# The opening of layer 0: fewer zero transfers, tables and statistics issued earlier

## The chip, the cores and the metric

The kernel runs on one core of a Trainium2 chip. The metric is device time in microseconds (us) of one execution, as the median of several runs. The core's engines are called PE (matrix products), DVE (vector), ACT (scalar) and POOL (GpSimd); SP only issues transfers. ACT and POOL issue transfers too. Sixteen DMA engines carry what these queues issue.

## The reference

The program is four residual layers over an image `x` of shape 2 x 192 x 96 x 96. Before each layer a group norm without weights is taken of each image. Only the beginning of layer 0 matters here:

```
def _gn(v, G=32, eps=1e-5):                      # per image, 32 groups of 6 channels
    return (g - mean) / sqrt(var + eps)
xr   = conv1x1(_gn(x), w_reduce, b_reduce)       # 192 -> 180 channels
offs = conv1x1(xr, w_offset, b_offset)           # 180 -> 360 channels: (y, x) shifts of samples
f_w  = deform_conv2d(xr, offs[:, :180], ...)     # 3x3, samples xr at shifted places
f_h  = deform_conv2d(xr, offs[:, 180:], ...)
x    = x + conv1x1(attention-weighted sum of f_w and f_h)
```

Layers 1 to 3 (a Laplacian with a 1x1 convolution, a two-way WKV scan, a state space scan) follow and are the same in both kernels.

## The kernel before

Layer 0 handles the two images one after the other. For each image it needs the group norm's scale and bias, so it must first read the whole image for statistics. Then the first projection, `reduce0`, makes for each of 72 tiles of 128 pixels the 180 channels and the 360 offsets in one product, and writes both to device memory: the pixels into `xp_d`, a frame of 106 x 106 pixels of 194 floats with zeros around the 96 x 96 picture, and the offsets into `o_d`, with zero rows at both ends. After that, `near0` samples and convolves image 0; image 1's projection is interleaved with that ("aside").

The order of the beginning, as the program states it in `layer0`:

1. `stats_of(x, 0, 0)`: six loads of 96 x 2 x 1536 floats on SP, 36 `bn_stats` on DVE (L127). `gn` (L95 to L109) makes scale and bias of them.
2. `reduce_constants`: loads of the projection's weights (L76), a transposed and fused weight `wall` (L197 to L238), and the zeros: DVE clears the tile `zero` (L240), and ACT's queue sends it to device memory, for each image two transfers into `o_d` with 97 rows each (L246), one transfer for each of the ten zero lines of `xp_d`, 106 rows of 776 bytes each (L251), and two of 96 rows for the left and right margins (L252, L256).
3. `reduce0` of image 0: the tile's load on SP (L269), the normalization on DVE (L114), four products on PE (L286), the bias added on DVE into `xk` (L296 to L300), and five transfers of `xk` on ACT's queue (L306, L314). `xk` has four buffers. The products' PSUM pool `r0p` has three.
4. `stats_of(x, 0, 1)` and `gn` for image 1.
5. `near_constants`: small tables made on DVE by chains of operations on 128 x 1 values (L352 to L402), with ramps from POOL (L339), the load `sb_b_off`, and the store of a table `where` to `at_d` (L408). It also holds the loads of the convolution's weights `wd`, `wl` on POOL's queue (L439).
6. `near0` of image 0. It starts with loads of `raw` from `o_d` (L488), windows `xw` from `xp_d` on POOL's queue (L543, 16 transfers for a tile), `u` = `raw` + table (L498), the hat functions `h` on POOL and ACT (L525, L532, L534) and their products `sp` on DVE (L555). From the first `sp` on, DVE works nearly without a break.

A tile framework turns this into one instruction stream for each engine. It orders outside `near0` by its own priorities, so independent instructions may be moved ahead. Pools that are opened one after the other use the same memory: the first instruction on a new pool's tile waits until the old pool's last readers, transfers included, are done. Every transfer that SP or ACT issues takes one of eight completion semaphores in turn; a transfer with the same semaphore as an earlier one is issued after the earlier one has landed.

Of the kernel before, what the change touches and what calls it, by code (L numbers as in the profile page):

```python
# [6 lines left out]
F32 = mybir.dt.float32  # L7
# [4 lines left out]
PSUM = bass.MemoryType.PSUM  # L12
# [4 lines left out]
B, C, H, W = 2, 192, 96, 96  # L17
# [5 lines left out]
NS = 2 * G * KK  # L23
PITCH = 106
FRAME = 4
CW = 194
# [35 lines left out]
class Net:  # L62
# [52 lines left out]
            out, x, sc[:, k : k + 1], bi[:, k : k + 1], ALU.mult, ALU.add  # L115
        )

    def stats_of(self, src, layer, b):
        nc, tc = self.nc, self.tc
        stats = self.new_stats(layer, b)  # L120
        with tc.tile_pool(name=f"st{layer}{b}", bufs=4) as sb:
            for n in range(0, N512, 3):
                xt = sb.tile([CH, 2, 3 * 512], F32, name="xt")
                nc.sync.dma_start(out=xt, in_=halves(src[b])[:, :, n * 512 : (n + 3) * 512])
                for i in range(3):
                    for k in range(2):
                        nc.vector.bn_stats(  # L127
                            stats[:, k, n + i, :], xt[:, k, i * 512 : (i + 1) * 512]
                        )
        return stats  # L130

    def layer0(self, x, out):
        nc, tc, ins = self.nc, self.tc, self.ins
        new = [self.new_stats(1, b) for b in range(B)]
        with ExitStack() as ctx:
            wp = ctx.enter_context(tc.tile_pool(name="w0", bufs=1))
            xp_d, o_d, f_d, u_d, top = [], [], [], [], []
            for b in range(B):  # L140
                xp_d.append(self.dram.tile([PITCH, PITCH, CW], F32, name=f"xp_d{b}"))
                o_d.append(self.dram.tile([OB + HW + OA, 2 * NS], F32, name=f"o_d{b}"))
                f_d.append(self.dram.tile([2, CM, HW], F32, name=f"f_d{b}"))
                u_d.append(self.dram.tile([NT * LT, 2 * NS], F32, name=f"u_d{b}"))
                top.append(wp.tile([P, 8], F32, name=f"top{b}"))
            at_d = self.dram.tile([NT * LT, 4], F32, name="at_d")
            far = wp.tile([1, B], I32, name="far")
            sums = [self.dram.tile([2, CM], F32, name=f"sums_d{b}") for b in range(B)]
            with tc.tile_pool(name="wn0", bufs=1) as wn:
                gns = [self.gn(0, 0, self.stats_of(x, 0, 0))]  # L150
                wall, bias = self.reduce_constants(wn, xp_d, o_d)
                with tc.tile_pool(name="r0", bufs=4) as sb, tc.tile_pool(
                    name="r0p", bufs=3, space=PSUM
                ) as ps:
                    for _ in self.reduce0(
                        x[0], gns[0], wall, bias, xp_d[0], o_d[0], sb, ps, "pr", nc.scalar
                    ):
                        pass
                gns.append(self.gn(0, 1, self.stats_of(x, 0, 1)))
                con = self.near_constants(wn, at_d)  # L160
                with tc.tile_pool(name="r1", bufs=2) as sb:
                    aside = (x[1], gns[1], wall, bias, xp_d[1], o_d[1], sb)
                    self.near0(0, xp_d[0], o_d[0], u_d[0], f_d[0], sums[0], far, top[0], con, aside)
                self.near0(1, xp_d[1], o_d[1], u_d[1], f_d[1], sums[1], far, top[1], con)
            for b in range(B):
                rv = nc.values_load(far[0:1, b : b + 1], min_val=0, max_val=1)
                with tc.If(rv > 0):
                    self.far0(b, xp_d[b], o_d[b], f_d[b], sums[b])
            we = ctx.enter_context(tc.tile_pool(name="we0", bufs=1))
            wex = self.load(  # L170
                "w_exp", [MH, 2, C], ins["w_exp"].rearrange("(k p) o -> p k o", k=2), we
            )
            bex = self.load("b_exp", [CH, 2], pool=we)
            wat = self.load(
                "w_attn", [MH, 2, 2], ins["w_attn"].rearrange("(k p) o -> p k o", k=2), we
            )
            bat = self.load("b_attn", [P, 2], rows_of(ins["b_attn"], P), we)
            for b in range(B):
                few = (top[b], at_d, u_d[b], xp_d[b])
                self.expand0(b, x, out, f_d[b], sums[b], few, wex, bex, wat, bat, new[b])  # L180
        return new

    def reduce_constants(self, wn, xp_d, o_d):
# [5 lines left out]
        with tc.tile_pool(name="wr0", bufs=1) as wr, tc.tile_pool(  # L189
            name="wrp0", bufs=2, space=PSUM  # L190
        ) as ps:
            wred = self.load_halves("w_red", CM, wr)
            bred = self.load("b_red", [MH, 2], pool=wr)
            row = self.load("b_red_row", [P, CM], rows_of(ins["b_red_row"], P), wr)

            for k in range(2):
                nc.vector.tensor_copy(  # L197
                    wall[:, k, :CM].rearrange("p (e q c) -> p e q c", e=2, c=CG),
                    wred[:, k].rearrange("p (q e c) -> p e q c", e=2, c=CG),
                )  # L200
            nc.vector.tensor_copy(
                bias[:, :CM].rearrange("p (e q c) -> p e q c", e=2, c=CG),
                row.rearrange("p (q e c) -> p e q c", e=2, c=CG),
            )

            raw = self.load(
                "w_off", [MH, 2, 2 * NS], ins["w_off"].rearrange("(k p) o -> p k o", k=2), wr
            )
            woff = wr.tile([MH, 2, 2 * NS], F32, name="woff")
            for k in range(2):  # L210
                for a in range(2):
                    for cv in range(2):
                        nc.vector.tensor_copy(
                            woff[:, k].rearrange(
                                "p (t a q c e) -> p a c t q e", t=KK, a=2, c=2, e=2
                            )[:, a, cv],
                            raw[:, k].rearrange(
                                "p (a c q e t) -> p a c t q e", a=2, c=2, t=KK, e=2
                            )[:, a, cv],
                        )  # L220
            for k in range(2):
                back = wr.tile([MH, 2, CH], F32, name="back")
                for m in range(2):
                    pt = ps.tile([P, 2 * NS], F32, name="pt")
                    nc.tensor.transpose(
                        pt[:MH, :CH], wred[:, k, m * MH : (m + 1) * MH], self.ident[:CH, :CH]
                    )
                    nc.vector.tensor_copy(back[:, m], pt[:MH, :CH])
                pt = ps.tile([P, 2 * NS], F32, name="pt")
                for m in range(2):  # L230
                    nc.tensor.matmul(pt[:CH], back[:, m], woff[:, m], start=m == 0, stop=m == 1)
                nc.vector.tensor_copy(wall[:, k, CM:], pt[:CH])
            many = wr.tile([MH, 2, P], F32, name="many")
            nc.vector.tensor_copy(many, bred.unsqueeze(2).to_broadcast([MH, 2, P]))
            pt = ps.tile([P, 2 * NS], F32, name="pt")
            for m in range(2):
                nc.tensor.matmul(pt, many[:, m], woff[:, m], start=m == 0, stop=m == 1)
            nc.vector.tensor_copy(bias[:, CM:], pt)  # L238
            zero = wr.tile([PITCH, 8 * NS], F32, name="zero")
            nc.vector.memset(zero, 0.0)  # L240
            F = FRAME
            end = PITCH - F - W
            for b in range(B):

                for lo, n in ((0, 2 * OB), (HW, OB + OA)):
                    nc.scalar.dma_start(  # L246
                        out=o_d[b][lo : lo + n].rearrange("(p r) c -> p (r c)", p=97),
                        in_=zero[:97, : n // 97 * 2 * NS],
                    )
                for y in (*range(F), *range(F + H, PITCH)):  # L250
                    nc.scalar.dma_start(out=xp_d[b][y], in_=zero[:, :CW])  # L251
                nc.scalar.dma_start(  # L252
                    out=xp_d[b][F : F + H, :F, :].rearrange("y x c -> y (x c)"),
                    in_=zero[:H, : F * CW],
                )
                nc.scalar.dma_start(  # L256
                    out=xp_d[b][F : F + H, F + W :, :].rearrange("y x c -> y (x c)"),
                    in_=zero[:H, : end * CW],
                )
# [1725 lines left out]
```

## Time and profile before

| | us |
|---|---|
| median of 3 runs (lowest to highest) | 12206.34 (12203.41 to 12206.52) |
| the profiled execution | 12226.28 |
| its span | 12224.5 |
| PE busy, share of the span | 10189.2, 83% |
| DVE busy | 9584.8, 78% |
| ACT busy | 6563.0, 54% |
| POOL busy | 6938.6, 57% |

The shares are averages over all four layers. What the change touches lies in the first 480 us, under 4% of the span, so it is read there, by stretches of the timeline. In the page's 40 slices this is the first slice and half of the second: PE has 3 tenths of the first and 5 of the second, against 9 in the slices after it.

### The profile page before, as it was taken

How to read it: one execution, taken by the hardware profiler on the slowest of the kernel's cores; microseconds unless marked ns; L12 is line 12 of the kernel's file. 1: busy time of each engine (PE TensorE's matmuls, PEld its weight loads, DVE VectorE, ACT ScalarE, POOL GpSimd, SP SyncE). 2: the span in 40 equal slices, each digit the busy share in tenths (PEclk: the TensorE clock that was granted, in tenths of full speed). 3: DMA queues.
4: the chain of work that ended last, by engine and by line, in shares of the span. 5: the costliest groups of instructions: out<-in, count | busy, mean ns of one | idle time of the engine just before them, and what ended most of it. 6: DMA issues, size and time to landing. Idle time of an engine off the chain costs nothing. (4 is left out here: it accounts for less than half of the span.)

```text
span 12224.5 us, 231723 instructions
## 1 busy us (share of the span) xinstructions
PE 10189.2 (83%) x89389; PEld 5830.4 (48%) x89389; DVE 9584.8 (78%) x10919; ACT 6563.0 (54%) x12866; POOL 6938.6 (57%) x6899
## 2 busy tenths in 40 slices
PE   3599999998999999967767777778888888888887
PEld 2488888887888888852222222222222222222222
DVE  3777777776777777765688777679889899888988
ACT  0366666665766666630026433356565656656565
POOL 0366666765666666631247433356666666666666
PEclk9899999999999999978867777789899898898989
DMA  4534444432333333334322111111111111111111
GB/s 107 93 93 96 96 95 96 99 94 71 83 89 91 92 91 92 91 94 127 101 92 97 55 43 50 38 43 44 45 41 46 39 44 45 41 45 40 44 45 38
DMA packets 596759, 875.84 MB, mean 72 GB/s; under 512 B 237184, under 2 KB 322492, under 8 KB 594624
## 3 DMA queue, kind: packets, MB, share of 16 engines
q1 hardware_dynamic: 373448, 659.98, 20.4%
q0 software_dynamic: 103808, 133.18, 5.1%
q10 hardware_dynamic: 118392, 67.73, 1.9%
q8 instruction: 714, 11.70, 0.4%
q14 instruction: 397, 3.25, 0.1%
HBM read 423.24 MB, written 187.60 MB: 50 GB/s over the span
## 5 line engine op out<-in xcount | busy, mean ns | idle before, releaser
L1849 POOL TENSOR_TENSOR bu<-du,bb 128x512 f32<-128x512 f32 x1728 | 2235.2, 1308 | 1293.5 <-DVE h L1852 1286.1
L1856 PE MATMUL acc<-hc,ident 128*128 128x512 f32 x3456 | 1939.2, 677 | 652.0 <-DVE hc L1855 652.0
L1852 DVE TENSOR_TENSOR_SCAN h<-da,state,bu 128x512 f32<-128x512 f32 x1632 | 2030.1, 1274 | 240.5 <-ACT da L1847 199.0
L555 DVE TENSOR_TENSOR sp<-h 128x2304 f32<-128x2304 f32 x790 | 2161.7, 2769 | 19.9 <-ACT h L534 19.9
L579 ACT COPY st<-pt 128x512 f32<-128x512 f32 (+1 forms) x2370 | 1217.7, 516 | 1306.3 <-PE pt L571 1236.9
L577 DVE COPY st<-pt 128x512 f32<-128x512 f32 x1580 | 1062.0, 687 | 981.8 <-PE pt L571 965.9
L571 PE MATMUL pt<-ident,sp 128*128 128x128 f32 x14220 | 1678.8, 276 | 126.7 <-DVE sp L555 79.0
L525 POOL TENSOR_TENSOR h<-u,step 128x1152 f32<-128x1152 f32 (+1 forms) x474 | 1208.0, 2562 | 816.5 <-DVE u L498 468.7
L571 PEld LDWEIGHTS pt<-ident,sp 128*128 128x128 f32 x14220 | 1565.1, 142 | 214.5 <-issue 89.1
L1856 PEld LDWEIGHTS acc<-hc,ident 128*128 128x128 f32 x3456 | 630.2, 203 | 1874.5 <-DVE hc L1855 1497.2
L543 POOL DMA_DIRECT2D xw<-xp_d x2500 | 1389.4, 633 | 179.5 <-PE pt L618 83.5
L1847 ACT ACTIVATE da<-dl,sb_A_log 128x512 f32<-128x512 f32 x1728 | 1184.4, 687 | 4.0 <-POOL dl L1834 0.7
L1855 DVE TENSOR_TENSOR hc<-h,cc 128x512 f32<-128x512 f32 x1728 | 1117.3, 678 | 21.9 <-DVE h L1852 0.5
L618 PE MATMUL pt<-st,xw 64*32 64x288 f32 (+1 forms) x30000 | 1074.0, 366 | 72.4 <-ACT st L579 26.6
L1853 ACT COPY state<-h 128x1 f32<-128x1 f32 x1728 | 321.4, 190 | 1496.8 <-DVE h L1852 1496.4
L639 ACT COPY val<-pt 128x288 f32<-128x288 f32 (+1 forms) x3132 | 985.1, 398 | 209.0 <-PE pt L618 204.2
L686 PE MATMUL pf<-more,wl 54*64 54x128 f32 (+1 forms) x17064 | 957.6, 268 | 11.2 <-DMA more<-val 10.2
L686 PE MATMUL pf<-main,wd 126*64 126x128 f32 (+1 forms) x17064 | 962.3, 270 | 0.6
L686 PEld LDWEIGHTS pf<-main,wd 126*64 126x64 f32 x17064 | 889.9, 137 | 140.4 <-issue 136.4
L686 PEld LDWEIGHTS pf<-more,wl 54*64 54x64 f32 x17064 | 919.6, 136 | 47.7 <-issue 33.5
L618 PEld LDWEIGHTS pt<-st,xw 64*32 64x32 f32 x30000 | 539.6, 106 | 478.8 <-ACT val L639 169.8
L1844 PE MATMUL cc<-xd,pick 16*128 16x512 f32 x1152 | 710.5, 699 | 0.0
(309 smaller groups left out, 13505.0 us busy)
## 6 DMA issues: line engine op xcount, KB each, us to landing
main<-val SPq DMA_DIRECT2D x2016, 81.0 KB
bb<-br SPq DMA_DIRECT2D x576, 256.0 KB
more<-val SPq DMA_DIRECT2D x1728, 40.5 KB
xw<-xp_d POOLq DMA_DIRECT2D x2500, 26.0 KB
xt<-x_d SPq DMA_DIRECT2D x108, 384.0 KB
u_d<-u SPq DMA_DIRECT2D x158, 180.0 KB
raw<-o_d SPq DMA_DIRECT2D x156, 180.0 KB
half<-half_d SPq DMA_DIRECT2D x54, 512.0 KB
```

The costliest lines, as they stand in the source:

```text
L525: nc.gpsimd.tensor_tensor(hs, u[:, :, 8 * KK * l : 8 * KK * l + n].unsqueeze(3).to_broadcast([P, 2, n, WS]), con["step"].unsqueeze(1).unsq ...
L543: nc.gpsimd.dma_start(out=xw[e * WN : (e + 1) * WN, i], in_=xp_d[y : y + WS, x : x + WS, e * CM // 2 : e * CM // 2 + XW],)
L555: nc.vector.tensor_tensor(sp.rearrange("p s (y x) -> p s y x", x=WS), hy.unsqueeze(3).to_broadcast([P, n, WS, WS]), hx.unsqueeze(2).to_bro ...
L571: nc.tensor.transpose(pt[:, q], sp[:, 2 * (q0 + q) : 2 * (q0 + q) + 2].rearrange("p e w -> p (e w)"), self.ident,)
L579: nc.scalar.copy(st[:, q0 : q0 + m], pt[:, :m])
L618: nc.tensor.matmul(pvs[e][lane : lane + 32, j * w : (j + 1) * w], xw[e * WN : (e + 1) * WN, win, g * CG : g * CG + 32], sts[pair][e * WN : ...
L686: nc.tensor.matmul(to, wt[:, m * CO : (m + 1) * CO], took.rearrange("p h (r c) -> p h r c", c=columns), start=first and l == 0 and t == 0, ...
L1847: nc.scalar.activation(da, dl[:, d], AF.Exp, scale=nA[:, d, n : n + 1])
L1849: nc.gpsimd.tensor_tensor(bu, du[:, d], bb, ALU.mult)
L1852: nc.vector.tensor_tensor_scan(h, da, bu, init, ALU.mult, ALU.add)
L1855: nc.vector.tensor_tensor(hc, h, cc, ALU.mult)
L1856: nc.tensor.matmul(acc[d], self.ident, hc, start=n == 0, stop=n == NST - 1)
```

## The change

Three things are edited.

- The ten zero lines of `xp_d` are cleared with two transfers for each image. The tile `zero` becomes 97 x 10282 floats (it was 106 x 1440), and the lines 0 to 3 go out as 8 rows of 10282 floats, the lines 100 to 105 as 12 rows.
- `near_constants` is called after the first image's statistics and ahead of its `gn`.
- `stats_of` becomes a generator that yields after each load with its six `bn_stats`. The second image's statistics are advanced from inside the loop over `reduce0`, every thirtieth yield (ten tiles) from the twentieth on, and their loads have two buffers instead of four. The PSUM pool of the projection gets six buffers instead of three.

```diff
-    def stats_of(self, src, layer, b):
+    def stats_of(self, src, b, stats):
         nc, tc = self.nc, self.tc
-        stats = self.new_stats(layer, b)
-        with tc.tile_pool(name=f"st{layer}{b}", bufs=4) as sb:
+        with tc.tile_pool(name=f"st{b}", bufs=4 - 2 * b) as sb:
             for n in range(0, N512, 3):
...
-        return stats
+                yield
...
-                gns = [self.gn(0, 0, self.stats_of(x, 0, 0))]
+                first = self.new_stats(0, 0)
+                for _ in self.stats_of(x, 0, first):
+                    pass
+                con = self.near_constants(wn, at_d)
+                gns = [self.gn(0, 0, first)]
                 wall, bias = self.reduce_constants(wn, xp_d, o_d)
                 with tc.tile_pool(name="r0", bufs=4) as sb, tc.tile_pool(
-                    name="r0p", bufs=3, space=PSUM
+                    name="r0p", bufs=6, space=PSUM
                 ) as ps:
-                    for _ in self.reduce0(
-                        x[0], gns[0], wall, bias, xp_d[0], o_d[0], sb, ps, "pr", nc.scalar
+
+                    second = self.new_stats(0, 1)
+                    others = self.stats_of(x, 1, second)
+                    for i, _ in enumerate(
+                        self.reduce0(
+                            x[0], gns[0], wall, bias, xp_d[0], o_d[0], sb, ps, "pr", nc.scalar
+                        )
                     ):
+                        if i % 30 == 20:
+                            next(others, None)
+                    for _ in others:
                         pass
-                gns.append(self.gn(0, 1, self.stats_of(x, 0, 1)))
-                con = self.near_constants(wn, at_d)
+                gns.append(self.gn(0, 1, second))
...
-            zero = wr.tile([PITCH, 8 * NS], F32, name="zero")
+            zero = wr.tile([97, PITCH // 2 * CW], F32, name="zero")
...
-                for y in (*range(F), *range(F + H, PITCH)):
-                    nc.scalar.dma_start(out=xp_d[b][y], in_=zero[:, :CW])
+                for lo, hi in ((0, F), (F + H, PITCH)):
+                    nc.scalar.dma_start(
+                        out=xp_d[b][lo:hi].rearrange("y (p q) c -> (y p) (q c)", q=PITCH // 2),
+                        in_=zero[: 2 * (hi - lo), : PITCH // 2 * CW],
+                    )
```

## The prediction

> **What bounds the kernel now.** The change lies before 480 us, so I read the waits of SP's queue first, then the timeline of that stretch engine by engine, then the DMA view of the zero transfers. Waits of SP's queue, in two stretches (total, times, longest):
>
> ```profile
> SPq L269 <- DMA xp_d<-zero: 113.8, 4, 110.0
> ...
> SPq L408 <- DVE base L379: 25.7, 1, 25.7
> SPq L269 <- DMA at_d<-where: 10.4, 1, 10.4
> ```
>
> The projection's first load (L269) waits 110 us for the zeros. The store of the table `at_d` waits 25.7 us for DVE's tables. And something behind that store waits until it has landed. The timeline (start, length, engine) places these:
>
> ```profile
> 47.05 3.65 DVE L127 BATCH_NORM_STATS2 stats<-xt 96x6 f32<-96x512 f32 x6 [4.48 <-DMA xt<-in_x]
> 50.73 1.14 DVE L95 BATCH_NORM_AGGREGATE mv<-stats 96x2 f32<-96x108 f32 x2
> 54.83 1.26 DVE L240 MEMSET zero<- 106x1440 f32 x1 [0.44 <-DVE gn_b L109]
> ...
> 56.18 3.49 ACTq L246 DMA_DIRECT2D o_d<-zero  x2
> 59.70 45.98 ACTq L251 DMA_DIRECT2D xp_d<-zero  x10
> ...
> 170.29 27.49 SPq L269 DMA_DIRECT2D xt<-in_x  x18
> ...
> 359.81 0.92 ACTq L314 DMA_DIRECT2D xp_d<-xk  x2
> 360.83 1.47 ACTq L306 DMA_DIRECT2D o_d<-xk  x3
> 362.40 1.13 ACTq L314 DMA_DIRECT2D xp_d<-xk  x2
> ...
> 384.13 16.50 SPq L124 DMA_DIRECT2D xt<-in_x  x6
> 419.99 1.14 DVE L95 BATCH_NORM_AGGREGATE mv<-stats 96x2 f32<-96x108 f32 x2
> ...
> 424.68 15.49 POOL L543 DMA_DIRECT2D xw<-xp_d  x28
> 449.38 0.41 SPq L408 DMA_DIRECT2D at_d<-where  x1
> 449.80 0.53 DVE L498 TENSOR_TENSOR u<-raw,base 128x360 f32<-128x360 f32 x1
> 459.51 5.03 DVE L555 TENSOR_TENSOR sp<-h 128x2304 f32<-128x2304 f32 x2 [1.23 <-ACT h L534]
> ```
>
> Four stretches in a row set the time of the first `sp`: statistics of image 0 (to 50.7), norm, constants and zeros (119.6, to 170.3), projection (213.8, to 384.1), statistics of image 1, tables and first hats (75.4, to 459.5). In the third, ACT issues a tile's five transfers in 0.92 + 1.47 us with gaps of 0.1 us, back to back: ACT's issue is its pace (72 tiles from 175.35 to 382.6, 2.88 us each).
>
> What takes 110 us in the zeros? The DMA view of 62 to 70 us, then of 102 to 106 us (packets, MB, share of 16 engines):
>
> ```profile
> q10 hardware_dynamic: 70, 0.20, 6.5%
> ...
> q10 hardware_dynamic: 204, 0.16, 14.1%
> ```
>
> In the first the 97-row transfers of L246 run on one engine (1/16 is 6.25%). In the second the 106-row lines run on two. In the packet records the one-engine part takes 11.0 + 21.4 = 32.4 us for an image, at 26 GB/s. The ten lines take 2.15 us each; 16.9 us (image 0) and 21.1 us (image 1) of them come after the one-engine part, the margins 3.1 and 1.9. With a bubble of 3.1 between the images and 0.7 at the end this makes 111.5 us from the first packet (58.8) to 170.3.
>
> **The change, part by part.** The instruction order of the changed kernel decides most of it. On DVE the tables' chain (158 instructions) stands behind all 36 `bn_stats` and ahead of the norm: it fills no wait for input.
>
> *Statistics of image 0.* POOL's ramps now stand behind 11 of the 20 weight loads and wait for the last statistics. So nine loads of 114 KB leave the stretch, which ran at 198 GB/s: -5 us; I take -4.5 (end at 46.2), since the 11 still share the first 35 us. Nothing early needs those weights.
>
> *Tables*: +25.6 us to the store of `at_d` (423.75 to 449.38), and +1 for `sb_b_off`, whose load now meets the nine weight loads (0 to 3).
>
> *at_d.* The norm's tiles take the tables' memory, so DVE waits at L95 for `at_d` to land, and SP's weight loads stand behind that too. Before, it was issued at 449.38, its 10112 packets of 16 bytes ended at 473.6, and the wait for it ended at 479.9: 30.5 us. That row is the price; low end 25.6 (last packet plus the 1.4 us that other loads show), high 33. +30.5.
>
> *Norm*: 3.7 as before, plus ACT's table load of 1.28 us, which now waits for the same product as the square root: +1.3. *Memset*: 1.26 us for 1440 elements makes 8.8 to 9.0 for 10282: +7.5.
>
> *Constants*: w_red to last bias took 15.2 us (54.46 to 69.65). They end some 75 us before the zeros, which cover them; without that cover they would cost about 15. ACT's fifth zero transfer waits for w_red's load by the semaphores' turn; the 32 us already in the first engine's queue cover that.
>
> *Zero chain.* The 97-row transfers stay, for both images on the same engine. Of the lines remain 8 and 12 rows of 41 KB. Here the row and a rule speak apart. The nearest row is the line transfer: two engines, 2.15 us for 82 KB, so 43 us for both images and nothing gained. The Trainium skill, DMA: Bandwidth & Descriptors, "Rules for kernel authors", speaks against the change: an outermost dimension under 16 confines a transfer to that many engines. Its section "Why a DMA increments its semaphore by 16 and not by 1" says a transfer uses the largest number up to 16 that divides the outer dimensions, always the lowest-numbered engines. This trace agrees for 97 (one) and 106 (two). So 8 and 12 rows get 8 and 12 engines, and the first carries one 41 KB row of each, 1.6 us at 26 GB/s, 6.3 for four. I take the rule. Chain: 64.8 + 6.3 + 5.0 + 0.7 = 76.8 instead of 111.5: -34.7. By the row, about +37 more.
>
> This stretch becomes 119.6 + 25.6 + 1 + 30.5 + 1.3 + 7.5 - 34.7 = 150.8: the zeros end at 197 instead of 170.
>
> *Projection.* The six loads (1152 KB) are pulled far ahead: the first stands behind four tile loads, all are read by tile 31. DVE carries 1.4 us for a tile plus one or two `bn_stats` of 0.61, under 2.9: free. More PSUM does nothing, as ACT sets the pace. But through the semaphores ACT waits for each load. The second is issued about 10.3 us after the stretch begins (after tile 4's load, itself behind the first, lands), and landing takes 9; ACT would want it at 14.1, gets it at 19.5: 5.4 us. Loads 3 to 6 are issued when DVE has used an older buffer, 3.6 us after tile n+9 starts on ACT, and ACT needs them at tile n+12, 9.1 us after it. Alone a load takes 6.2 + 1.4 us; beside ACT's writes (DMA share 0.61) 8 to 9. Stall 2.5 to 4 each. Sum +18; from 0, if they land in time, to 50, if ACT waits out each landing.
>
> *First hats.* Statistics, norm and tables (384.1 to 449.8) go. What is late next is POOL: 16 of the 32 windows stand ahead of `h`, 16 x 0.553 = 8.9 us, then `h` 2.6, ACT 2.4: first `sp` 14.4 us after the projection instead of 75.4: -61. `raw` and the norm (4 us) lie beside. Afterwards POOL's `xk` waited 23 us, until 479.9, with hats behind it, and DVE idled 3.5 + 2.2 us: -4.5.
>
> Sum: -4.5 + 31.2 + 18 - 65.5 = -20.8 us. Against the profiled execution's 12226.3 that is 12205.5; the median stands 20 us lower, so 12185. Everything later keeps its order.
>
> **Rivals.**
> - *It does what it says* (0.08): the tables hide and the norm does not wait. Then 26.6 + 30.5 us less: 12128. Against it: the order on DVE and its wait at L95.
> - *The loads land in time* (0.13): no stall, 12167. For it: DMA share 0.61, and the loads are issued two or three tiles ahead. Against: 8 to 9 us of landing for 5.5 us of lead.
> - *Slower* (0.10): the lines' transfers run on one engine, as the 97-row ones do. Then their 1.65 MB at 26 GB/s take 63 us instead of 6.3, in the zero chain: 12241. It decides from 51 us of chain on, that is below 32 GB/s. Against it: 106 rows took two engines.
> - *Own forecast* (0.69): 12185, own range 12160 to 12210.
>
> **How the numbers follow.** About 0.2% (24 us) is what a measurement of this kernel can tell from no change: limits 12182 and 12231. My forecast lies just inside; with +/-15 us it gives 0.27 faster, 0.41 same, 0.01 slower. The first two rivals are faster (0.21), the third slower (0.10). Together 0.48, 0.41, 0.11. The range, 12142 to 12232, leaves out the first rival and most of the third.
>
> **What would show it.** L95 starts near 103 us, behind `at_d`; the memset takes 9 us; the first projection load comes near 197 (140 for the first rival, 250 for the third). Of the line transfers, 8 and 12 engines work. The projection takes 232 us, with ACT's issue gaps behind the statistics' loads before tile 31 only. The first `sp` comes 14 us after the last transfer of `xk`. I am wrong if L95 does not wait for `at_d`, or if ACT's gaps exceed 30 us.

## The result

Over 12 runs of each the changed kernel took 12206.84 us (12188.16 to 12224.79), the kernel before 12207.14 us (12185.86 to 12233.78): ratio 0.9997, interval 0.9988 to 1.0006. That is no change that this comparison can tell. A second comparison (21 runs against 57, told below) gave 0.9989 (0.9982 to 0.9995), which is a gain of 13 us, with 6 and 22 as ends. The first one allows from 15 us less to 7 us more. A gain of some 13 us, a tenth of a per cent, lies in both intervals; only the second one tells it from none. In the changed kernel's profile (span 12223.0 us, execution 12224.79 us) the first `sp` comes at 447.7 instead of 459.5.

### The profile page after: what moved, and what is told of

It is laid out like the page before. It is cut to its first block, busy times and chain, and to the rows that moved or that the text cites. A ratio compares the mean times of both kernels' runs of the same rounds, so it can differ in the third digit from the quotient of the medians.

```text
span 12223.0 us, 231699 instructions
## 1 busy us (share of the span) xinstructions
PE 10225.7 (84%) x89389; PEld 5843.6 (48%) x89389; DVE 9589.2 (78%) x10919; ACT 6562.3 (54%) x12866; POOL 6934.5 (57%) x6899
## 5 line engine op out<-in xcount | busy, mean ns | idle before, releaser
L631 PE MATMUL pt<-st,xw 64*32 64x288 f32 (+1 forms) x30000 | 1072.3, 366 | 73.3 <-ACT st L592 27.4
```

What stands on the lines that cost most here:

```text
L631: nc.tensor.matmul(pvs[e][lane : lane + 32, j * w : (j + 1) * w], xw[e * WN : (e + 1) * WN, win, g * CG : g * CG + 32], sts[pair][e * WN : ...
```

## The profile after

Waits (engine, line, what was waited for: total, times, longest), from those of SP's queue up to 490 us:

```profile
SPq L282 <- DMA o_d<-xk: 111.9, 54, 8.6
SPq L282 <- DMA o_d<-zero: 84.5, 2, 62.3
...
SPq L76 <- DMA at_d<-where: 29.4, 1, 29.4
SPq L421 <- DVE base L392: 25.6, 1, 25.6
```

The projection's first loads (L282) wait 62.3 and 22.2 us for the zeros where one wait took 110. In its place stand two that were not there so early: 25.6 for the tables and 29.4 for the landing of their store. The timeline shows where (start, length, engine, line):

```profile
43.11 3.65 DVE L126 BATCH_NORM_STATS2 stats<-xt 96x6 f32<-96x512 f32 x6 [0.77 <-DMA xt<-in_x]
46.84 0.06 DVE L365 MEMSET at<- 128x1 f32 x1
...
72.38 0.40 SPq L421 DMA_DIRECT2D at_d<-where  x1
102.25 1.14 DVE L95 BATCH_NORM_AGGREGATE mv<-stats 96x2 f32<-96x108 f32 x2 [29.49 <-DMA at_d<-where]
105.32 1.28 ACT L107 ACT_TABLE_LOAD   x1 [105.32 <-PE pv L105]
109.53 8.63 DVE L250 MEMSET zero<- 97x10282 f32 x1 [2.28 <-issue]
...
118.24 2.38 ACTq L256 DMA_DIRECT2D o_d<-zero  x2
120.65 15.25 ACTq L261 DMA_DIRECT2D xp_d<-zero  x2
...
198.65 1.79 SPq L282 DMA_DIRECT2D xt<-in_x  x4
...
430.94 0.91 ACTq L327 DMA_DIRECT2D xp_d<-xk  x2
...
434.05 8.92 POOL L556 DMA_DIRECT2D xw<-xp_d  x16 [11.20 <-DMA xp_d<-xk]
442.80 5.64 POOL L538 TENSOR_TENSOR h<-u,step 128x1152 f32<-128x1152 f32 x3
447.69 3.17 DVE L568 TENSOR_TENSOR sp<-h 128x2304 f32<-128x2304 f32 x1 [5.86 <-ACT h L547]
```

The first table instruction (L365) starts 0.08 us after the last statistics: none of the 158 fills a wait for input. DVE then stands 29.5 us at L95. First projection load 198.65 against 170.29: +28.4. The projection, from that load to the end of the last `xk` issue, took 233.2 us against 212.4 (170.29 to 382.64): +20.8. From there to the first `sp` 15.8 against 76.9: -61.0. Sum -11.8.

The rest of the program can be followed by matching instructions in the two traces, counted from the end. The lead (how much earlier the changed kernel starts the same DVE instruction) is 14.6 us at 580 us and 13.7 at 5.15 ms, then 18.2 at 7.06 ms, 4.4 at 8.44 ms and 1.5 at the end. What changed it lies between 7.3 and 8.0 ms, in a stretch that the diff doesn't touch. The view by stretches, first before, then after, then a second profile of the changed kernel (bounds, length, busy time with instructions of PE, PEld, DVE, ACT, POOL; then granted clock, DMA share, GB/s):

```profile
7300.00:8000.00 700.00, 524.86 (x909) 144.60 (x908) 488.17 (x522) 238.73 (x372) 218.98 (x211) 0.72 0.15 43
```

```profile
7300.00:8000.00 700.00, 533.43 (x891) 146.16 (x890) 476.53 (x512) 239.60 (x371) 213.84 (x207) 0.69 0.15 43
```

```profile
7300.00:8000.00 700.00, 508.50 (x907) 142.69 (x906) 493.72 (x531) 259.17 (x400) 236.15 (x223) 0.73 0.15 44
```

The granted clock was 0.72 and 0.69 there, with PE busy three quarters of the time. In the second profile it was 0.73, and the lead went the other way, from 11.4 us at 7.06 ms to 32.0 at 8.44 ms and 26.0 at the end. So this stretch shifted these single executions by 14 and 21 us, in opposite directions: it is not a gain given back by the change. That the clock is what shifts it fits the three rows, but three profiles don't show it.

## The experiments

The runs were made in four groups: the three parts with the repetition; od_48 to stats_pool; spread with the two last versions; pieces. Each group has its own runs of the kernel before, with medians of 12223.67, 12220.76, 12224.69 and 12210.32 us, and each ratio is against those of its group.

### The three parts alone

```diff
 zeros_only:  before + zero 97 x 10282, lines in two transfers per image
 stats_only:  before + the generator and the loop over reduce0 (r0p 6, two buffers); tables after gn of image 1
 tables_only: before + con = self.near_constants(wn, at_d) between statistics and gn of image 0
 all_again:   the changed kernel
```

> The kernel before with the zeros of the changed kernel alone (a 97 x 10282 tile, the frame's lines in two transfers per image). Own theory (8 and 12 engines carry the lines, the 97-row transfers stay on one): zero chain 111.5 -> 79 us, memset +7.4, so the first projection load comes at 145 (170.3 before) and the first sp at 434 (459.5 before), 25 us earlier; whole time -0.2%. Rival (few long lines run on one engine or are no faster): first load at 178 or later, whole time +0.05% or more. Rival (the zeros were hidden anyway): first load unchanged at 170.

> The kernel before with the second image's statistics among the tiles of the first projection alone (tables still after them, zeros as before). Own theory: the 36 us between projection and norm go away, the projection takes 19 us longer while the six loads are in flight; first load stays at 170, last transfer of xk 402 (384 before), first sp at 442 (459.5 before): -17 us. Rival (statistics cost what they save): projection over 245 us, first sp at 459 or later. Rival (they fit into idle time): projection 214, first sp at 423.

> The kernel before with the tables' call alone moved between the first statistics and the first norm. Own theory: tables (25.6) and the landing of at_d (30) stand ahead of norm, constants and zeros, 4.5 come back because nine weight loads leave the first statistics: first projection load at 223 (170.3 before), +53; after the projection 26 less: first sp at 486, +27; whole time +0.15 to +0.2%. Rival (the tables run while DVE waits for input, as their place suggests): first load at 170, first sp at 434, -26. Rival (at_d's landing is not waited for): first load at 193, first sp at 456.

> The changed kernel again, beside its parts. If the parts add up: -25 -17 +27 = -15 us at the first sp against -11.8 in the profile shown, and a median ratio of 0.9985 to 1.000. Theory that the gain is given back later in the program by a rule (a later stage that waits for something of its own): first sp 12 us earlier, end within 3 us of before in the profile again. Theory that only the granted clock of the later stages hid it: the lead at the end differs from the lead at 580 us by the clock of that profile, either way.

| kernel | first projection load | projection | first `sp` | against 459.5 | ratio to before (interval) |
|---|---|---|---|---|---|
| before | 170.3 | 212.4 | 459.5 | | |
| zeros_only | 146.8 | 209.9 | 432.8 | -26.7 | 0.9976 (0.9967 to 0.9985) |
| stats_only | 188.6 | 209.5 | 439.5 | -20.0 | 0.9986 (0.9979 to 0.9993) |
| tables_only | 221.5 | 211.2 | 484.4 | +24.9 | 1.0020 (1.0012 to 1.0027) |
| all_again | 199.9 | 234.2 | 450.2 | -9.3 | 0.9989 (0.9982 to 0.9995) |

The ratios times 12224 us make changes of -29, -17, +24 and -13 us. The lead at the first `sp` lies within each interval, so it reaches the end. So two parts of the change gain and the third takes half of it back. One line of tables_only's waits says why:

```profile
DVE mv L95 <- DMA at_d<-where: 27.8, 1, 27.8
```

The parts sum to -21.8, the whole gives -11.8 and -9.3. The missing 10 us are in the place of the statistics. My expectation for stats_only was wrong in its steps, though -20 is near the -17 expected (first load 188.6, not 170; projection 209.5, not 19 us longer): with nothing to hold them, SP's queue took the second image's loads ahead of the projection, beside the zeros:

```profile
50.42 0.31 SPq L123 DMA_DIRECT2D xt<-in_x  x1
...
55.95 119.06 SPq L123 DMA_DIRECT2D xt<-in_x  x5
188.61 50.16 SPq L279 DMA_DIRECT2D xt<-in_x  x28
```

They cost the zeros 18.3 us there and the projection nothing. In the whole they run during the projection and cost it 20.8, or 27.4 against the sum of the parts' projections (each is 1 to 3 us shorter than before's).

### The zero chain

```diff
-                        out=o_d[b][lo : lo + n].rearrange("(p r) c -> p (r c)", p=97),
-                        in_=zero[:97, : n // 97 * 2 * NS],
+                        out=o_d[b][lo : lo + n].rearrange("r c -> (r c)").rearrange("(p f) -> p f", p=48),
+                        in_=zero[:48, : n * 2 * NS // 48],
```

> The changed kernel with the zeros of o_d laid out as 48 equal rows instead of 97 (same addresses). Theory (97 rows run on one engine, and both images' 12.3 + 21 us of them are in the zero chain): chain from first issue to first projection load 80.5 -> 45 us, first load at 164 (199 now), first sp at 413 (449 now). Rival (the queue moves no more than some 60 GB/s of zeros however they are laid out): 4.86 MB at 60 GB/s is 80 us, nothing gained, first load at 199.

The DMA view of this stretch in 40 slices (tenths of 16 engines, then GB/s), first the changed kernel from 118 to 199 us, then this one from 118 to 162:

```profile
DMA  0000000099049051200000000000901863211100
GB/s 6 17 26 26 26 24 26 28 168 107 20 89 164 38 188 47 101 26 41 12 20 27 26 24 26 24 28 26 249 26 48 130 112 119 102 68 78 43 9 14
...
q10 hardware_dynamic: 920, 4.81, 29.1%
```

```profile
DMA  0999999300498003223936999930039930331320
GB/s 0 259 217 202 181 192 123 37 0 0 43 260 131 0 0 114 92 86 141 239 66 175 222 255 181 144 37 0 0 37 208 152 37 0 89 135 62 133 93 30
...
q10 hardware_dynamic: 784, 4.81, 67.7%
```

The same 4.81 MB. In the first view the stretches of the digit 0 are the 97-row transfers alone, at 26 GB/s on one engine of 16; with 48 rows they and the lines beside them start at some 200 GB/s. The chain from first issue to first projection load went from 80.4 to 44.1 us, the first `sp` to 412.2, the time to 0.9957 (0.9944 to 0.9970). The theory's 164 and 413 were met within 2 us (162.3 and 412.2), and the rival (nothing gained) fails.

### The landing, and whose memory the tables take

```diff
 where_apart:
-            where = tmp.tile([P, NT, 4], F32, name="where")
+            where = wn.tile([P, NT, 4], F32, name="where")
 tables_apart:
-        with tc.tile_pool(name="pl0", bufs=1) as tmp:
+        for tmp in (wn,):
```

> The changed kernel with the tile behind at_d's store (where) in memory of its own, so that the norm's tiles do not take its place. Theory (the norm waits for that landing, 29 to 30 us): L95 at 73, first projection load at 169 (199 now), first sp at 420 (449 now); the store then lands beside norm and memset and costs nothing. Rival (the 10112 packets of 16 bytes hold up the weight loads behind them on SP's queue all the same): constants and zeros 20 us or more later than the norm, first load at 190.

> The changed kernel with all tiles of the tables' function in memory of their own; the place of the call is unchanged. Theory (the tables stand behind the last statistics only because their tiles take the memory of the statistics' input tiles): about half of them run between the statistics, the statistics end at 50 (nine weight loads come back), L95 at 51, norm and memset to 67 with some tables between, first projection load at 147 (199 now), first sp at 397 (449 now), ratio to before 0.995. Rival (DVE has no room there: 22 us of statistics and 26 of tables in 46 us): L95 at 65 or later, first load at 165.

DVE's and SP's lines of where_apart:

```profile
71.75 0.40 SPq L421 DMA_DIRECT2D at_d<-where  x1
...
72.17 1.14 DVE L95 BATCH_NORM_AGGREGATE mv<-stats 96x2 f32<-96x108 f32 x2
...
178.24 1.79 SPq L282 DMA_DIRECT2D xt<-in_x  x4
```

L95 no longer waits: 30 us. A third of it was lost again, as the zero chain is 90.1 us (88.16 to 178.24) instead of 80.4. It now starts beside the store's packets (72.7 to 96.3): ACT's first two zero transfers take 8.1 us to issue, until 96.3, against 2.4, and the next two 19.0 against 15.3. The theory had the landing cost nothing; it cost 10 us. The rival fails too: the first zero transfer comes 16.0 us after L95, as in the changed kernel. First load 178.2, not 169, first `sp` 430.3, not 420; ratio 0.9977 (0.9966 to 0.9988).

With all table tiles in memory of their own, and the call where the change put it, the tables (L415) do run between the statistics (L126):

```profile
22.81 3.65 DVE L126 BATCH_NORM_STATS2 stats<-xt 96x6 f32<-96x512 f32 x6 [2.79 <-DMA xt<-in_x]
...
26.84 0.30 DVE L415 TENSOR_TENSOR where<-at,corner 128x144 f32<-128x144 f32 x1
...
31.10 3.66 DVE L126 BATCH_NORM_STATS2 stats<-xt 96x6 f32<-96x512 f32 x6 [3.32 <-DMA xt<-in_x]
...
50.82 0.63 DVE L95 BATCH_NORM_AGGREGATE mv<-stats 96x2 f32<-96x108 f32 x1
```

So the pool was the reason that they stood behind the statistics. The rival (no room on DVE) fails: L95 at 50.8. But the first projection load came at 173.4, not at 147, because `at_d`'s store now fell beside the zeros. ACT's lines:

```profile
93.99 21.68 ACTq L256 DMA_DIRECT2D o_d<-zero  x2
121.50 21.75 ACTq L261 DMA_DIRECT2D xp_d<-zero  x2
169.24 0.33 ACTq L265 DMA_DIRECT2D xp_d<-zero  x1
```

In the packet records the store's 10112 packets of 16 bytes last from 85.9 to 167.4 here, 82 us; nearly alone, in the changed kernel, they took 21.5 (73.3 to 94.8). ACT's next transfer (L265, at 169.24) is issued 1.8 us after the last of them. The trace's semaphores tell what it waited for: the one of the store, which came free at 169.2, 26.0 us after ACT's transfer before. Those 26 us are about what lies between 147 and 173.4. First `sp` 422.9, not 397; ratio 0.9970 (0.9958 to 0.9981).

### Why the projection got longer

My prediction had it that ACT waits for each load through the eight semaphores. Three kernels went after that:

```diff
 stats_pool: the changed kernel, image 1's six statistics loads on POOL's queue
+        queue = nc.gpsimd if b else nc.sync
...
-                nc.sync.dma_start(out=xt, in_=halves(src[b])[:, :, n * 512 : (n + 3) * 512])
+                queue.dma_start(out=xt, in_=halves(src[b])[:, :, n * 512 : (n + 3) * 512])
 spread: the changed kernel, each of these loads tied to a tile
+                if after:
+                    nc.vector.tensor_copy(xt[:, 0, 0:1], after[0][:CH, 0:1])    # after[0]: the tile's xk
 pieces: as spread, loads of 512 columns instead of 1536, four buffers
-                        if i % 30 == 20:
+                        if i % 9 == 5:
```

> The changed kernel with the second image's six statistics loads issued by POOL instead of SP. Theory (ACT's transfers stall because SP's and ACT's transfers share eight semaphores in turn, and a 1.2 MB load holds its turn for 8 to 9 us): the projection takes 214 to 218 us (233 now), first sp at 431 (449 now). Rival (the loads take the transfers' bandwidth): the same bytes in the same stretch, 228 us or more, first sp within 5 us of now.

> The changed kernel with each of the second image's six statistics loads tied to a tile of the projection (one element copied from that tile's xk into the load's buffer first), one for each ten tiles instead of six in the first 85 us. Theory (six loads, 7.08 MB, meet a projection that leaves about 48 GB/s of the 181 GB/s it reached with them: 4 MB find room in 85 us, the rest costs 17 us): spread over 180 us they find room, projection 214 to 219 us (233 now), first sp at 434 (449 now). Rival (each load delays its neighbours by the same 3 us wherever it stands): 228 us or more, first sp within 5 us of now.

> The kernel of the spread experiment with the second image's statistics loads cut into 18 of 0.39 MB, each tied to every third tile, four buffers. Spread over the stretch and moved to another queue, six loads of 1.18 MB still cost 20 us, 3.3 us each. Theory (a load of 1.18 MB keeps the transfers busy some 6.5 us, longer than the four buffers of xk can bridge, and ACT, whose issue is the pace, has no reserve to make up a lost microsecond): a third of it, 2.2 us, is bridged; projection 213 to 220 us (233 now), first sp at 434 (448 now). Rival (each byte has its price, 2.8 us per MB, in pieces of any size): 230 us or more, first sp within 4 us of now. Rival (each transfer that joins the turn of eight costs): 18 of them, 240 us or more.

Projection: 234.6 us (stats_pool), 232.7 (spread), 224.0 (pieces), against 233.2 and 234.2 in the changed kernel. The first `sp` came at 449.0, 445.3 and 436.2, where 431, 434 and 434 were expected; ratios to before 0.9995 (0.9987 to 1.0003), 0.9986 (0.9976 to 0.9995) and 0.9984 (0.9975 to 0.9993).

In stats_pool the loads no longer take a semaphore of the eight that SP and ACT use in turn. The sum is the same as before, but 9.3 us of it lie at another place: POOL's two first loads delayed the first `xk` transfer to 14.5 us after the first load, 5.2 in the changed kernel. The rest, 13 us over before's 212.4, are stops of ACT:

```profile
212.56 0.80 ACTq L328 DMA_DIRECT2D xp_d<-xk  x2
...
226.94 5.89 ACTq L320 DMA_DIRECT2D o_d<-xk  x3
...
233.51 0.34 DVE L310 TENSOR_TENSOR xk<-pr,bias 128x180 f32<-128x180 f32 x1 [5.61 <-DMA o_d<-xk]
```

The semaphores in the traces tell what ACT's transfers waited for (waits of 0.1 us and more, summed over the projection). In the changed kernel it is 5.7 us for statistics loads (9.0 in its second profile) and 11.1 us (7.9) for ACT's own earlier `xk` transfers, which land later beside the loads; in the kernel before these were 0.2 us. In stats_pool they are 12.3 us, in spread 19.8, and no wait is for a statistics load. So ACT does stop in the turn of eight, but for the most part at its own transfers; taking the loads out of the turn doesn't help.

Spread over the stretch the loads cost as much as bunched, so it is not the mean load of the transfers either, though that fell in the rows shown. Rows of 205 to 240 us, the changed kernel, then spread, then pieces (last columns: granted clock, DMA share, GB/s):

```profile
205.00:240.00 35.00, 24.82 (x88) 19.39 (x87) 19.93 (x61) 0.00 (x0) 0.88 (x8) 0.80 0.85 181
```

```profile
205.00:240.00 35.00, 31.24 (x121) 24.64 (x120) 22.18 (x75) 0.00 (x0) 1.11 (x10) 0.90 0.71 159
```

```profile
205.00:240.00 35.00, 29.99 (x122) 23.39 (x120) 23.28 (x79) 0.00 (x0) 1.11 (x10) 0.95 0.80 175
```

In spread the tiles' distance on ACT is 2.6 to 3 us for most tiles, and 6.9, 6.5, 5.5, 5.5, 5.3 and 4.7 once behind each load. So each load costs 2 to 4 us wherever it stands, and ACT, whose issue sets the pace, never makes it up. In pieces the distance behind a load is 3.2 to 4.2, and half of the price is gone (11.6 us over before's 212.4 instead of 20 to 22). Both my theory (213 to 220) and its rivals (230 or more, 240 or more) miss that. The size of a load is one half of the cause. The other half is again ACT's wait for its own `xk` transfers, 11.1 us in 15 stops of at most 1.4; whether it goes with the bytes or with the number of loads stays open.

### Versions beyond both

```diff
 moved, against spread (in words, except for the lines of code):
+ reduce_constants first, its tiles and a zero tile of 96 x 5141 in a pool open until the projection ends
+ near_constants behind the first tile of the loop, its tiles in wn
+ zeros of image 0 on ACT behind the last statistics: 48 rows for o_d, 16 and 24 rows of 5141 for the lines
+ zeros of image 1 on SP after the second statistics, inside the projection
+ if i % 27 == 14:   next statistics load
-            nc.sync.dma_start(out=at_d.rearrange("(n p) c -> p n c", p=P), in_=where)
+            nc.sync.dma_start(out=at_d.rearrange("(p n) c -> p n c", p=P), in_=where)
+ and its reader gathers row lane * NT + tile
 moved_pool, against moved:
-                queue.dma_start(out=xp_d[FRAME + y, ...
+                nc.gpsimd.dma_start(out=xp_d[FRAME + y, ...
```

> All in one: constants and the zero tile at the start, tables in memory of their own and behind the first tile, zeros of image 0 in full-width rows after the last statistics, those of image 1 in the projection, statistics loads tied to every ninth tile, at_d stored by lane (128 pieces of 1264 bytes, read back by another row number). If the terms measured one by one add up: statistics to 50, norm to 55, zeros of image 0 (2.43 MB at 110 GB/s) to 75, projection 214 from 65: last xk transfer at 280 to 290, first sp at 300 (459.5 in the kernel before), -160 us, ratio 0.987. Rival (the crowded start costs DVE and the queues what it saves): first sp at 360 or later, ratio 0.992 or more.

> The same with the projection's xp_d transfers (two of five per tile) issued by POOL instead of ACT. Theory (ACT's issue of 2.88 us a tile is the projection's pace): ACT needs 1.6 us a tile, DVE 1.9, the transfers' 383 KB 2.1 at 181 GB/s, and the statistics' 7.08 MB and image 1's 2.4 MB of zeros now cost 50 us of it: projection 200 us, first sp 285, 10 to 20 us before the kernel without this. Rival (POOL's issue is slower or meets DVE): projection 214 us or longer.

moved: 0.9905 (0.9890 to 0.9920), first `sp` 342.3, not 300. Its start went nearly as worked out (L95 at 52.8, first load 59.2), and the store of `at_d` became 128 packets that took 0.6 us. But its projection took 267 us, not 214: the first `xk` transfer left at 78.1, 19 us after the first load, as two of ACT's zero transfers waited 14.2 and 4.5 us for tile loads in the turn of eight; and tiles are 5 to 6 us apart behind each statistics load again, and up to 8 around image 1's zeros. moved_pool: 12060.82 us against 12224.69, ratio 0.9863 (0.9848 to 0.9878), 164 us less than before and the fastest kernel here. The end of the projection, first in moved, then in moved_pool with its first load and its first `sp`:

```profile
318.56 1.48 ACTq L328 DMA_DIRECT2D o_d<-xk  x3
320.13 0.92 ACTq L336 DMA_DIRECT2D xp_d<-xk  x2
321.15 1.47 ACTq L328 DMA_DIRECT2D o_d<-xk  x3
```

```profile
59.40 20.01 SPq L290 DMA_DIRECT2D xt<-in_x  x13
...
276.29 1.01 POOL L336 DMA_DIRECT2D xp_d<-xk  x2 [0.69 <-DVE xk L319]
...
278.11 1.05 POOL L336 DMA_DIRECT2D xp_d<-xk  x2 [0.67 <-DVE xk L319]
...
279.93 1.01 POOL L336 DMA_DIRECT2D xp_d<-xk  x2 [0.78 <-DVE xk L319]
...
299.55 3.16 DVE L577 TENSOR_TENSOR sp<-h 128x2304 f32<-128x2304 f32 x1 [6.18 <-ACT h L556]
```

Two of the five transfers of a tile on POOL's queue bring the first `sp` forward by 42.7 us, more than the 10 to 20 expected. At the end, where only tiles are under way and ACT waits for no landing in either kernel, they are 1.82 us apart instead of 2.6 to 2.9, which ACT fills back to back in moved. That ACT's issue is the pace there is shown by this. Over the whole projection two things are mixed: POOL's transfers also take semaphores of a set of their own, so they leave ACT's turn of eight, and this was not tried apart. The projection took 222 us (59.4 to 281.8), not 200; 15 of them went in one stop behind image 1's zeros. By its number the rival (214 or longer) came true too, but not in its sense (no gain), as moved takes 267.

## Why the prediction was right, and where it was off

The range held. It is 90 us wide and holds a kernel without any change too, so that alone says little, and of the two comparisons the first leaves -20.8 us out and the second just takes it in (-22). What speaks for the account are the stages: of the forecast -20.8 us the profile shows 14.6. The mechanism was right but for the projection, where the size was near and the reason only in part right; that is luck. Step by step, forecast against this profile:

- Statistics end at 46.8 (46.2 forecast), the store of `at_d` is issued 25.6 later as forecast; the extra 1 us for `sb_b_off` did not come. L95 at 102.25 (103), behind `at_d` by 29.5 (30.5). Norm 5.0 with ACT's table load of 1.28 in it: as forecast.
- *Memset*: 8.63 us, as worked out, but it started 2.28 us after the norm instead of 0.44. The gap also stands in zeros_only (2.29) and not in tables_only (0.44), so it comes with the larger tile. This 1.8 us is the term that was left out of the zeros' sum; why the gap is there was not tried.
- *Zero chain*: 80.4 from issue to load (before: 114.1), so -33.7 (forecast -34.7). The rule of the Trainium skill that I took against the nearest row (DMA: Bandwidth & Descriptors, "Why a DMA increments its semaphore by 16 and not by 1") held: two line packets of 41128 bytes for an image, those of the first engine by the rule, took 1.52 us each behind the 97-row part, and the other 18 ran beside it. By the row nothing would have been gained. zeros_only shows the gain by itself. First load at 198.65 (197).
- *Projection*: +20.8 (forecast +18). The size was near, the reason only in part right: I had ACT wait for each load to land. It did so for 5.7 us; 11.1 us more went in waits for its own transfers, which land later beside loads of 1.18 MB, on a queue that has no reserve. ACT's gaps over 4 us stand behind the loads and before tile 31 only, as forecast. That the added PSUM buffers bring nothing was argued, not tried alone.
- *First hats*: 15.8 us after the last `xk` issue (14.4), -61.0 as forecast. *near0's start*: the lead grew from 11.8 to 14.6 by 580 us, so -2.8 instead of -4.5.

What is missing from 20.8 is thus 1.7 at the first load, 2.8 in the projection and 1.7 in near0: 14.6. Of the rivals, "it does what it says" needed the tables' own memory: tables_apart has it and then meets the store; where_apart removes the norm's wait alone. "The slower case", lines on one engine, is refuted by zeros_only. "Loads land in time" is refuted by the projection's 233.2.

Nearly half of my chance lay on a gain beyond 24 us. The first comparison shows none, and the second one's interval ends at 22.

## What to carry to other kernels

A call that is moved earlier is early only if its tiles' memory is free early: ask whose memory a pool takes and which transfer still reads there. A table that the rest needs much later can hold up the norm by 29.5 us through a store that nobody reads yet.

Of a transfer, look at the rows first: 97 rows moved at 26 GB/s, the same bytes in 48 rows with nine tenths and more of all 16 engines at work while they ran.

Where one queue's issue sets the pace, work put beside it isn't free even if all engines have time left: a stop isn't made up. Two things helped here: to give part of the issues to another queue (-42.7 us at the first `sp`), and to cut the loads beside it into smaller ones (-9 us).

## What the runs showed of the hardware beyond what I had expected

- A store of 10112 packets of 16 bytes took 21.5 us when nearly alone and 82 us beside the zeros; laid out as 128 packets of 1264 bytes, its packets took 0.6 to 0.7 us.
- Nine and more of the 41128-byte packets at once took 6.4 us each on average, against 1.52 us for each of those behind the 97-row part. The highest GB/s that the rows of this stretch show for all transfers together is 249 (260 in od_48).
- A single statistics load of 1.18 MB cost the projection about 3.4 us on SP's queue, bunched or spread; cut in three it cost about half. On POOL's queue the sum was 22 us for the six, but 9 of them were a later first transfer.
- A transfer on ACT's queue stood 26.0 us for the semaphore of a store that SP had issued (tables_apart).
